# q/k projections of an attention image moved into the image itself, and another split of one convolution tile

## The chip, the cores and the metric

One core of a Trainium2 chip runs the whole kernel. The metric is device time in microseconds (us) of one execution; a run is several executions, and the median stands for them. The engines are called by the profile's names: PE (TensorE matmuls), PEld (its weight loads, which lie beside the matmuls), DVE (VectorE), ACT (ScalarE), POOL (GpSimd) and SP (SyncE, here only a DMA queue).

## The reference, cut to what matters

The input x has 16 images of 384 channels and 32 x 32 pixels. Each image passes two residual layers, all in float32:

```
x = x + attention(groupnorm(x))      # 8 heads of 48, over 1024 pixels; q, k, v, proj
x = x + dwconv7x7(groupnorm(x))      # one symmetrised 7x7 filter per channel
```

Attention is softmax(q kT / sqrt(48)) v for each head, and a projection with a bias. The convolution has 49 taps per channel, with a border of three zeros. Group norm works over 32 groups of 12 channels.

## The kernel before, in words

**Tiles.** An image is three tiles of 128 channels x 1024 pixels (k = 0, 1, 2). Heads go in four pairs (u = 4b + 0..3). For three pairs q and k are projected directly: qk_step(b, t, s) runs twelve float32 matmuls for pair t and s = 0 (q) or 1 (k) into a PSUM buffer (L415), and ACT copies it to the tile qk (L422). The fourth pair is gathered from spare rows of the first three by six SP DMAs (qk_rest, L431). In the profile each float32 matmul has two records.

**Blocks.** The main loop walks an image in eight blocks of eight steps (r = 0, 8, ..., 56; 16 steps are a pair). A block is eight s_steps (scores, L466, and the exp on ACT, L474), then a middle, then eight av_steps (L482) and one ACT copy of the accumulator (take, L493). Values v (v_step, L441) are projected in the middle of the block r = 0; the output projection of the image in front (project, proj_step, L535) follows there. The instruction streams of all engines are in order.

**Order.** A planner in Python writes the order: clock is PE's planned time, vclock that of DVE. catch_up(to) puts DVE work (convolution taps, and delayed calls of after(wait, cost, f)) into the stream until vclock reaches clock. act_slot(free) puts ACT work that is due (a first-in first-out list, applies) into the stream if its cost fits. other(done, scores_next) stands in the middle and at the end of each block and places a projection or q/k chunks. Due times are planned, not measured: an engine that gets there early waits.

**Images.** There is one x buffer (xpool, bufs = 1). begin_x(b + 1) loads the next image into it once the last reader of image b is in the stream: before, that is the last v_step, since q and k of image b were all projected during image b - 1 (`queue(b + 1)`, chunks 0 and 1 behind project, the others at fixed blocks). x_apply normalises the three tiles in place on ACT (L332), and had its place in the middle of project.

**Convolution.** x1_chains(b, st) normalises the attention's output (xn, L332) and starts its taps: one scalar_tensor_tensor on DVE per tap and tile (conv_tap, L600), up to three tiles in turn. Four of the last six tiles go to PE instead: PE_TILES = (14, 2), (14, 1), (15, 2), (15, 1). Each of their halves (16 image rows, 512 columns) is two pieces of 28 matmuls (conv_on_pe, L705) in four groups of 32 output channels; it reads two shifted copies sh that eight DMAs bring back from DRAM (conv_load, L682), issued by SP and ACT in turn. conv_on_pe_end adds the PSUM buffer to DVE's sum (L720), and a POOL DMA writes it out (L613). The tile SHARED = (14, 1) is divided: DVE takes the upper half, PE the lower one (h = 1). So PE's convolution is seven half tiles, in this order, here H1 to H7: (14,2) h0 and h1, (14,1) h1, (15,2) h0 and h1, (15,1) h0 and h1. The copies sh live in the pool qkpool (five buffers, one of them for a weight matrix), so a half's two copies are loaded when the half two places in front of it has been computed. PSUM tiles of this kind come from a pool of three (ps_s). Tile (15, 0), LONE, stays on DVE with two sums in turn (sum2) that are added at the end (L860).

**The two ends.** At the start eight warm matmuls of 384 columns (L1045) run on PE before the statistics of image 0 are averaged there (groups_on_pe, L301, two rounds); then x is normalised (L328 and L332) and all six qk_steps of image 0 follow. At the end come the last divisions (L563, L564), projection (L572), residual (L581), group norm on PE, and the convolution pieces.

Of the kernel before, what the change touches and what calls it, by code (L numbers as in the profile page):

```python
# [13 lines left out]
ALU = mybir.AluOpType  # L14
# [30 lines left out]
def kernel(  # L45
# [64 lines left out]
    def run(general):  # L110
        tag = "g" if general else "f"
        with ExitStack() as stack:
# [20 lines left out]
            def psum(name):  # L133
                return ps_s.tile([P, 2, HALF], F32, tag="s", name=name)
# [4 lines left out]

            PE_TILES = [(b, k) for b in (B - 2, B - 1) for k in PE_K]  # L140
            SHARED = None if general else (B - 2, PE_K[1])
            LONE = (B - 1, 0)

            def flat(t):
# [2 lines left out]
            def halves(t):  # L147
                return t.rearrange("p (h n) -> p h n", h=2)
# [444 lines left out]
            def conv_tap(b, k, dy, dx, dst=None):  # L593
                (oy, iy), (ox, ix) = region(dy, dx)
                if (b, k) == SHARED:
                    oy = slice(oy.start, min(oy.stop, H // 2))
                    iy = slice(iy.start, oy.stop - oy.start + iy.start)
                dst = x1s[b, k] if dst is None else dst
                acc = dst.rearrange("p (h w) -> p h w", w=W)[:, oy, ox]
                nc.vector.scalar_tensor_tensor(  # L600
                    acc,
                    xn1s[b, k].rearrange("p (h w) -> p h w", w=W)[:, iy, ix],
                    wsym[:, k, dy + PAD, dx + PAD : dx + PAD + 1],
                    acc,
                    ALU.mult,
                    ALU.add,
                )
# [84 lines left out]
            def conv_on_pe(b, k, h, part):  # L692
                if (b, k) not in pss:
                    pss[b, k] = psum(f"ps_conv_{b}_{k}")
                order = sorted(
                    ((d0, dx) for d0 in range(2) for dx in range(-PAD, PAD + 1)),
                    key=lambda t: t[1] != 0,
                )
                for n, (d0, dx) in enumerate(order):
                    if n // KS != part:  # L700
                        continue
                    _, (ox, ix) = region(0, dx)
                    for i in range(SH):
                        src = shs[b, k, h, i // 2][:, i % 2, 0 : ROWS * W]
                        nc.tensor.matmul(  # L705
                            pss[b, k][CH * i : CH * (i + 1), h, :].rearrange(
                                "p (y x) -> p y x", x=W
                            )[:, :, ox],
                            lhsT=mats[k][:, i, d0 * KS + dx + PAD, :],
                            rhs=src.rearrange("p (y x) -> p y x", x=W)[  # L710
                                :, SH * d0 : SH * d0 + H // 2, ix
                            ],
                            start=(n == 0),
                            stop=(n == len(order) - 1),
                        )

            def conv_on_pe_end(b, k):
                h = slice((b, k) == SHARED, 2)
                dst = halves(x1s[b, k])[:, h]
                nc.vector.tensor_tensor(dst, pss.pop((b, k))[:, h], dst, ALU.add)  # L720
                conv_end(b, k)

            def exact_step(u, i):
# [95 lines left out]
            def us_tap(dy, dx):  # L819
                late_us = 0.02 if clock > last_image else 0.0  # L820
                rows = H - abs(dy)
                if tuple(active[0][0:2]) == SHARED:
                    rows = H // 2 - max(0, -dy)
                return (rows * (W - abs(dx)) + (128 if len(active) > 1 else 268)) / 955 + late_us

            def tap():
# [60 lines left out]
            def issue(c):  # L887
                nonlocal clock
                kind, b, i = c
                if kind == "qk":  # L890
                    qk_step(b, *divmod(i, 2))
                    clock += US_QK
                elif kind == "rest":
                    qk_rest(b)
                else:
                    v_step(b, i)
                    clock += US_V
                    if i == NT // 2 - 1 and b + 1 < B:
                        begin_x(b + 1)

            lims = []

            applies, pending = deque(), []
            ON_VECTOR = (B - 2,)

            def project(b):
                nonlocal clock
                for o in range(NK):
                    proj_step(b, o)
                    clock += US_PROJ  # L910
                    if b in ON_VECTOR:
                        after(8.0, 1.3, lambda o=o: x1_part(b, o))

                    if o == 1 and pending:
                        pending.pop()()
                if b not in ON_VECTOR:
                    after(1.6, 0.2, lambda: x1_means(b))
                if chunks and b + 2 in ready:

                    issue(chunks.popleft())  # L920
                    catch_up(clock)
                    act_slot(9.0)
                    issue(chunks.popleft())

            def x1_part(b, k):
# [40 lines left out]
            def act_slot(free):  # L966

                while applies and applies[0][0] <= clock and applies[0][1] <= free:
                    _, cost, f = applies.popleft()
                    free -= cost  # L970
                    f()
# [20 lines left out]
            def begin_x(b):  # L992
                load_x(b)
                if b == 1:
                    after(10.0, 3.8, lambda: x_channels(b))
                else:
                    pending.append(lambda: x_apply(b, None))

            def x_channels(b):
                st = Stats(f"x_{b}")  # L1000
# [34 lines left out]
                if p == NP - 1:  # L1035
                    proj.append((now() + 7.0, b))

            def queue(b):
                chunks.extend(("qk", b, i) for i in range(6))
                chunks.append(("rest", b, 0))  # L1040


            warm = psum("warm")
            for n in range(8):
                nc.tensor.matmul(  # L1045
                    warm[:, n % 2, 0:C], lhsT=v[:, n, 0:P], rhs=v[:, n, 0:C], start=True, stop=True
                )
# [8 lines left out]
            conv_weights()  # L1056
            means_of(st.bs, x_mean[:, 0, :])
            ready[0] = 0.0
            queue(0)
            every = [(b, k) for b in range(2, B) for k in range(NK)]  # L1060
            for n, bk in enumerate(every):
                after(3.0 * n, 0.0, lambda bk=bk: stream_in(*bk))
# [42 lines left out]
            def conv_piece():  # L1105
                nonlocal clock
                b, k, h, part = pe_conv.popleft()
                while (b, k, h, 1) not in shs:
                    loads(1)
                conv_on_pe(b, k, h, part)  # L1110
                clock += 6.2
                if part == 1:
                    loads(2)
                if (h, part) == (1, 1):
                    after(6.0, 1.2, lambda: conv_on_pe_end(b, k))

            def other(done, scores_next):

                catch_up(clock)
                if proj and proj[0][0] <= clock:  # L1120
                    project(proj.popleft()[1])
                elif scores_next and chunks:
                    kind, cb, i = chunks[0]
                    first = {"qk": 2 * NT * (i // 2), "rest": 2 * NT * 3}[kind]
                    if ready.get(cb, 1e9) <= clock and done >= first:

                        act_slot(9.0)
                        issue(chunks.popleft())
                        if kind == "qk":
                            issue(chunks.popleft())  # L1130
                catch_up(clock)

            def fast_finish(b):
# [27 lines left out]
            for b, n0, size in [  # L1161
# [2 lines left out]
                r = n0 - b * PER_B  # L1164
                if n0 == NS - PER_B:
                    last_image = clock
                if r == 0:
                    while chunks:
                        issue(chunks.popleft())
                    if b + 1 < B:  # L1170
                        queue(b + 1)
                for n in range(n0, n0 + size):
                    s_step(n)
                clock += (size * US_STEP + US_TURN) / 2
# [4 lines left out]
                if ending:  # L1179
                    catch_up(clock)  # L1180
                    divide_at_once(NP * b + NP - 1, 0)
                    vclock += 4.2
                    for o in range(NK):
                        proj_part(b, o, (0, 1))
                    clock += 2 * US_PROJ
                else:
                    catch_up(clock)
                    act_slot(4.5)
                    other(r + size, False)
                for n in range(n0, n0 + size):  # L1190
                    av_step(n)
                    u, h, i = n // (2 * NT), n // NT % 2, n % NT
# [5 lines left out]
                if ending:  # L1198
                    catch_up(clock)
                    assert not invs and not waiting  # L1200
                    fast_finish(b)
                else:
                    other(r + size, True)
                if b == B - 4 and r == 32:
                    after(0.0, 2.0, check_early)
                if b == 1 and r == 0:
# [88 lines left out]
```

## Time and profile before

| | us |
|---|---|
| median of 6 runs | 2933.49 |
| lowest and highest | 2931.82, 2935.51 |
| profiled execution | 2933.9 |
| its span, first to last instruction | 2932.0 |
| PE busy in it | 2910.4 (99%) |
| DVE busy | 2559.7 (87%) |
| ACT busy | 1434.0 (49%) |
| POOL busy | 192.6 (7%) |

A busy PE row says only that one matmul or another was under way; its ends are modelled. The mean granted PE clock is 0.996 of full speed. In the timeline a row is a merged group: its start, its length, the engine, the line, the operands, how often (x), and in brackets the idle time before it and what ended it. In the view by stages each engine has its busy time and, in brackets, its instructions; PEclk is the granted clock.

### The profile page before, as it was taken

The numbers are of one execution on the slowest core, as the hardware profiler recorded it, in microseconds if no ns is written. First come the engines' busy times: TensorE is split into PE (matmuls) and PEld (weight loads), VectorE is DVE, ScalarE is ACT, GpSimd is POOL, SyncE is SP. The second block draws the span as 40 slices with busy tenths as digits, with TensorE's granted clock in tenths as the row PEclk, the third lists the DMA queues.
The fourth block names the chain that finished last, engine by engine and source line by source line (L and its number), as shares of the span: only waits on it lengthen the run. The fifth ranks groups of instructions, "written<-read, shape, count | busy, mean of one in ns | idle before, by whom it ended". The sixth has DMA issues, their size and how long they took to land.

```text
span 2932.0 us, 30301 instructions
## 1 busy us (share of the span) xinstructions
PE 2910.4 (99%) x11562; PEld 1175.5 (40%) x11562; DVE 2559.7 (87%) x2565; ACT 1434.0 (49%) x1713; POOL 192.6 (7%) x305
## 2 busy tenths in 40 slices
PE   8999999999999999999999999999999999999998
PEld 4334343433434334343433434334343433434333
DVE  4500998989989898998989999898998999899997
ACT  2544545555454554545454454555445465454610
POOL 2213000010000001000000000001000000100000
PEclk9999999999999999999999999999999999999999
DMA  6513121121212112121121213013121221202324
GB/s 230 182 25 66 24 66 38 32 73 26 57 37 67 37 34 73 24 64 37 49 56 27 57 37 74 30 34 78 25 58 37 55 49 27 69 25 53 108 60 117
DMA packets 72540, 169.86 MB, mean 58 GB/s; under 512 B 30416, under 2 KB 32352, under 8 KB 70848
## 3 DMA queue, kind: packets, MB, share of 16 engines
q0 software_dynamic: 29456, 96.10, 12.0%
q1 hardware_dynamic: 41168, 68.12, 9.6%
q10 hardware_dynamic: 1760, 3.61, 0.5%
q8 instruction: 93, 1.52, 0.2%
q14 instruction: 63, 0.52, 0.1%
HBM read 119.93 MB, written 29.36 MB: 51 GB/s over the span
## 4 chain that ended last, share of the span: by engine, by line
PE 86%; DVE 7%; issue 5%; DMA 1%; POOL 0%; ACT 0%; POOLq 0%; SPq 0%; DVEq 0%; ACTq 0%
PE ps_s L466 27%; PE acc L482 27%; PE ps_qk L415 16%; PE ps_v L441 8%; PE ps_proj L535 7%; DVE x L600 6%; DVE sum L600 1%; PE warm L1045 0%; DVE o L518 0%; DMA out<-x 0%; DMA inv<-inv 0%; DMA gr_x<-af_x 0%; DVE bs_x L233 0%; PE ps_st_x L301 0%; ACT sq_x L264 0%
## 5 line engine op out<-in xcount | busy, mean ns | idle before, releaser
L600 DVE SCALAR_TENSOR_TENSOR x<-xn,wsym,x 128x899 f32<-128x899 f32 (+11 forms) x2181 | 2352.4, 1152 | 147.6 <-ACT xn L332 147.6
L474 ACT ACTIVATE e<-ps_s 128x1024 f32<-128x1024 f32 x1024 | 952.4, 1051 | 53.7 <-PE ps_s L466 50.8
L466 PE MATMUL ps_s<-qk 48*128 48x512 f32 x4096 | 914.2, 596 | 0.0
L482 PE MATMUL acc<-e,v 128*64 128x512 f32 x4096 | 907.2, 595 | 0.0
L466 PEld LDWEIGHTS ps_s<-qk 48*128 48x128 f32 x4096 | 376.5, 185 | 533.8 <-ACT e L474 257.7
L482 PEld LDWEIGHTS acc<-e,v 128*64 128x64 f32 x4096 | 282.9, 137 | 608.3 <-issue 603.7
L415 PE MATMUL ps_qk<-x,wqk 128*128 128x512 f32 x1152 | 507.2, 597 | 2.4 <-DVE x L328 2.4
L493 ACT COPY o<-acc 128x512 f32<-128x512 f32 x128 | 75.2, 588 | 672.8 <-PE acc L482 672.8
L415 PEld LDWEIGHTS ps_qk<-x,wqk 128*128 128x128 f32 x1152 | 217.0, 191 | 289.0 <-issue 286.5
L441 PE MATMUL ps_v<-wv,x 128*128 128x384 f32 x768 | 252.0, 488 | 0.0
L535 PE MATMUL ps_proj<-o,wp 128*128 128x512 f32 x540 | 234.2, 592 | 0.0
L422 ACT COPY qk<-ps_qk 128x1024 f32<-128x1024 f32 x96 | 96.8, 1009 | 257.9 <-PE ps_qk L415 257.9
L441 PEld LDWEIGHTS ps_v<-wv,x 128*128 128x128 f32 x768 | 144.6, 190 | 109.7 <-ACT e L474 12.1
L535 PEld LDWEIGHTS ps_proj<-o,wp 128*128 128x128 f32 x540 | 102.6, 190 | 125.9 <-issue 120.3
L450 ACT COPY v<-ps_v 128x384 f32<-128x384 f32 x128 | 55.1, 483 | 185.5 <-PE ps_v L441 185.5
L154 POOL DMA_DIRECT2D x<-in_x x42 | 22.3, 538 | 1645.6 <-PE ps_v L441 1608.3
L543 ACT ACTIVATE x<-ps_proj,bp 128x1024 f32<-128x1024 f32 x45 | 50.1, 1114 | 135.2 <-PE ps_proj L535 135.2
L518 DVE TENSOR_TENSOR o<-o,inv 128x1024 f32<-128x1024 f32 x63 | 76.8, 1218 | 37.6 <-DMA inv<-inv 34.9
L332 ACT ACTIVATE xn<-x,sc_x 128x1024 f32<-128x1024 f32 x46 | 53.8, 1235 | 87.7 <-DMA sc_x<-gr_x 63.8
L705 PE MATMUL ps_conv<-sh,mat 128*32 128x480 f32 (+3 forms) x784 | 83.1, 580 | 0.2 <-DMA sh<-xd 0.2
L507 DVE RECIPROCAL rec<-sums 128x16 f32<-128x16 f32 x63 | 15.4, 244 | 72.4 <-DMA sums<-sum 72.4
L355 DVE BATCH_NORM_STATS2 bs_all<-xs 128x6 f32<-128x512 f32 x84 | 51.7, 680 | 11.7 <-DMA xs<-in_x 11.7
(113 smaller groups left out, 522.0 us busy)
## 6 DMA issues: line engine op xcount, KB each, us to landing
x<-in_x POOLq DMA_DIRECT2D x90, 512.0 KB, 5.3
inv<-inv SPq DMA_DIRECT2D x126, 256.0 KB
out<-x POOLq DMA_DIRECT2D x48, 512.0 KB, 3.8
xs<-in_x POOLq DMA_DIRECT2D x42, 512.0 KB, 6.3
qk<-qk SPq DMA_DIRECT2D x96, 128.0 KB
o<-o SPq DMA_DIRECT2D x90, 64.0 KB
sh<-xd SPq DMA_DIRECT2D x34, 160.0 KB
sh<-xd ACTq DMA_DIRECT2D x22, 160.0 KB
```

What stands on the lines that cost most here:

```text
L415: nc.tensor.matmul(ps[:, h, :], lhsT=wqk[:, k, s, t, :], rhs=xns[b][:, k, h * HALF : (h + 1) * HALF], start=(k == 0), stop=(k == NK - 1),)
L422: nc.scalar.copy(halves(qks[u][:, s, :]), ps)
L441: nc.tensor.matmul(ps[:, j, 0:C], lhsT=xns[b][:, k, t * P : (t + 1) * P], rhs=wv[:, k, :], start=(k == 0), stop=(k == NK - 1),)
L450: nc.scalar.copy(dst.rearrange("p (h d) -> p h d", d=D + 1)[:, :, 0:D], ps[:, j, 0:C].rearrange("p (h d) -> p h d", d=D),)
L466: nc.tensor.matmul(ps[:, j, :], lhsT=qks[u][r, 1, i * P : (i + 1) * P], rhs=qks[u][r, 0, h * HALF : (h + 1) * HALF], start=True, stop=True,)
L474: nc.scalar.activation(es[n], ps, AF.Exp, scale=SCALE)
L482: nc.tensor.matmul(accs[u, h][64 * j : 64 * j + 64, :], lhsT=v_of(u, i, j), rhs=e[:, j, :], start=(i == 0), stop=(i == NT - 1),)
L493: nc.scalar.copy(os_[u][:, h * HALF : (h + 1) * HALF], accs.pop((u, h)))
L518: nc.vector.tensor_tensor(os_[u], os_[u], invs.pop(u), ALU.mult)
L535: nc.tensor.matmul(ps[:, h, :], lhsT=wp[:, t, o * P : (o + 1) * P], rhs=os_[NP * b + t][:, h * HALF : (h + 1) * HALF], start=(t == 0), sto ...
L600: nc.vector.scalar_tensor_tensor(acc, xn1s[b, k].rearrange("p (h w) -> p h w", w=W)[:, iy, ix], wsym[:, k, dy + PAD, dx + PAD : dx + PAD + 1],
L705: nc.tensor.matmul(pss[b, k][CH * i : CH * (i + 1), h, :].rearrange("p (y x) -> p y x", x=W)[:, :, ox], lhsT=mats[k][:, i, d0 * KS + dx + ...
```

## The change

Three things are changed.

1. **q and k.** A chunk is now one pair (both qk_steps). Only pair 0 of image b + 1 is projected during image b, from the block that ends at step 40 on. Pair 1 is projected in its own image, behind project (image 0: at the end of the block r = 0), and pair 2 at the end of the block r = 8. qk_rest and begin_x(b + 1) come behind pair 2, so the next image's load moves from behind v_step to there, and x_apply from the middle of project to the first slot from 7.0 us (planned) after that. Between the two steps of each pair there are now a catch_up and an act_slot. Image 0 starts its scores after pair 0 alone; image 15 now holds two pairs.
2. **The shared tile.** SPLIT = 24: DVE's taps on tile (14, 1) cover 24 of its 32 image rows instead of 16, and PE's pieces of H3 the last 8 rows, so its matmuls have 256 columns (less at the sides) instead of 512. Their number, 56, and the loads of sh stay. The last add covers 256 columns. The planned time of a piece of H3 is 3.2 instead of 6.2.
3. **Warm-up.** Four warm matmuls instead of eight.

```diff
+            SPLIT = 3 * H // 4
...
                 if (b, k) == SHARED:
-                    oy = slice(oy.start, min(oy.stop, H // 2))
+                    oy = slice(oy.start, min(oy.stop, SPLIT))
...
+                y0 = SPLIT - H // 2 if (b, k) == SHARED else 0
...
-                            )[:, :, ox],
+                            )[:, y0:, ox],
                             lhsT=mats[k][:, i, d0 * KS + dx + PAD, :],
                             rhs=src.rearrange("p (y x) -> p y x", x=W)[
-                                :, SH * d0 : SH * d0 + H // 2, ix
+                                :, SH * d0 + y0 : SH * d0 + H // 2, ix
                             ],
...
-                h = slice((b, k) == SHARED, 2)
-                dst = halves(x1s[b, k])[:, h]
-                nc.vector.tensor_tensor(dst, pss.pop((b, k))[:, h], dst, ALU.add)
+                c = slice(SPLIT * W if (b, k) == SHARED else 0, N)
+                dst = x1s[b, k][:, c]
+                nc.vector.tensor_tensor(dst, flat(pss.pop((b, k)))[:, c], dst, ALU.add)
...
                 if kind == "qk":
-                    qk_step(b, *divmod(i, 2))
-                    clock += US_QK
-                elif kind == "rest":
-                    qk_rest(b)
+                    act_slot(9.0)
+                    for s in range(2):
+                        qk_step(b, i, s)
+                        clock += US_QK
+                        if s == 0:
+
+                            catch_up(clock)
+                            act_slot(9.0)
+                    if i == NK - 1:
+                        qk_rest(b)
+                        if b + 1 < B:
+                            begin_x(b + 1)
                 else:
                     v_step(b, i)
                     clock += US_V
-                    if i == NT // 2 - 1 and b + 1 < B:
-                        begin_x(b + 1)
...
-                    if o == 1 and pending:
-                        pending.pop()()
...
-                if chunks and b + 2 in ready:
-
-                    issue(chunks.popleft())
-                    catch_up(clock)
-                    act_slot(9.0)
+
+                if chunks and chunks[0] == ("qk", b + 1, 1):
                     issue(chunks.popleft())
...
-                    pending.append(lambda: x_apply(b, None))
+                    applies.append((now() + 7.0, 3.7, lambda: x_apply(b, None)))
...
+            for b in range(B):
+                chunks.extend(("qk", b, t) for t in range(NK))
...
-            for n in range(8):
+            for n in range(4):
...
-            queue(0)
+            issue(chunks.popleft())
...
-                clock += 6.2
+                clock += 3.2 if (b, k) == SHARED else 6.2
...
-                    kind, cb, i = chunks[0]
-                    first = {"qk": 2 * NT * (i // 2), "rest": 2 * NT * 3}[kind]
-                    if ready.get(cb, 1e9) <= clock and done >= first:
-
-                        act_slot(9.0)
+                    _, cb, t = chunks[0]
+                    when = PER_B * cb + (-24, 8, 16)[t]
+                    if ready.get(cb, 1e9) <= clock and done >= when:
                         issue(chunks.popleft())
-                        if kind == "qk":
-                            issue(chunks.popleft())
...
-                if r == 0:
-                    while chunks:
+                if r % (2 * NT) == 0 and r // (2 * NT) < NK:
+                    while chunks and chunks[0][1:] <= (b, r // (2 * NT)):
                         issue(chunks.popleft())
-                    if b + 1 < B:
-                        queue(b + 1)
```

## The prediction

> **What bounds the kernel now.** I read the page first, then PE's waits, then the timelines of the first 60 us, of one image in the middle and of the last 110 us, and there the view of the loads.
>
> ```profile
> span 2932.0 us, 30301 instructions
> PE 2910.4 (99%) x11562; PEld 1175.5 (40%) x11562; DVE 2559.7 (87%) x2565; ACT 1434.0 (49%) x1713; POOL 192.6 (7%) x305
> ```
>
> ```profile
> PE warm L1045 <- POOL v L181: 5.1, 1, 5.1
> PE ps_qk L415 <- DVE x L328: 2.4, 1, 2.4
> PE ps_st_x L301 <- DVE d_x L316: 1.3, 2, 0.6
> PE ps_conv L705 <- DMA sh<-xd: 0.2, 1, 0.2
> PE ps_proj L572 <- DVE o L564: 0.2, 1, 0.2
> ```
>
> These are all of PE's waits (total, number, longest). None lies between 18.9 and 2826 us: PE runs without a gap through all sixteen images. Moving q/k work among images leaves its sum alone and can't win time there; it can only lose some if a gap opens. What can be won lies before 18.9 us, and in the tail, by taking matmuls away. In the middle DVE has room:
>
> ```profile
> 1691.80 3.68 DVE L600 SCALAR_TENSOR_TENSOR x<-xn,wsym,x 128x1024 f32<-128x1024 f32 x3 [9.87 <-ACT xn L332]
> ```
>
> The bracket is the idle time before the row: DVE has ended one image's taps 9.87 us before the next may begin. It is not behind.
>
> **The start.**
>
> ```profile
> 8.95 0.17 DVE L310 COPY mn_x<-st_x 128x3 f32<-128x3 f32 x1
> 9.07 2.87 PEld L1045 LDWEIGHTS warm<-v 128*128 128x128 f32 x9 [0.30 <-issue]
> 12.40 1.62 PE L301 MATMUL ps_st_x<-mn_x,masks 128*128 128x1 f32 x14
> 18.90 33.14 PE L415 MATMUL ps_qk<-x,wqk 128*128 128x512 f32 x72 [2.38 <-DVE x L328]
> 52.08 1.01 ACT L422 COPY qk<-ps_qk 128x1024 f32<-128x1024 f32 x1 [4.14 <-PE ps_qk L415]
> ```
>
> The means are ready at 9.12; L301 starts at 12.40, behind the warm matmuls. Weight loads come every 0.64 us up to 9.07, then nine in 2.87, so every 0.32. Eight records fewer are 8 x 0.32 = 2.56 us, and L301 could start at 9.8. Everything up to 18.90 is a chain behind it (PE, DVE, POOL, DVE), and the weights have landed by 14.3 (the view of transfers shows none from then to 19), so the first q/k matmul comes 2.56 earlier. Bounds: 2.9 at most, where DVE's means set it; at worst -0.6, if the shorter warm-up leaves PE at half clock for L301. The row for that is L301's second round in the tail, 3.06 for 14 loads instead of 1.64, twice 1.4 against the 2.2 still won.
>
> The clock matters again at 18.9:
>
> ```profile
> 16.20:22.80 6.60, 4.22 (x7) 2.07 (x8) 4.11 (x11) 1.24 (x1) 4.36 (x7) 0.50 0.54 180
> 2839.00:2845.60 6.60, 6.50 (x34) 4.04 (x38) 3.35 (x6) 1.24 (x1) 2.61 (x2) 0.50 0.14 32
> ```
>
> The 0.50 is the granted clock: after a spell of little PE work it is half for some 6.8 us. The first q/k matmuls lose about 2 us by that in either kernel; I take no difference (bounds 0.4 won, 1.4 lost). The Trainium skill ("TensorE: Matmul & The Clock Gate", Part 1: The HAM clock gate) says that full clock is granted after about 3.4 us of sustained work, counted in free-running windows. Four matmuls at 1.28 us are 5.1 us, which need not hold a whole window; by that rule the warm-up's gain is lost in part of the executions, and an estimate of its mean is half the 2.56. The trace shows full clock from 9.3, 4.2 us after the first, on which I rely.
>
> New: with pair 0 alone, the first score waits for ACT's copy of k. Before, PE went from q/k (whose last matmul ends at 52.04) straight to scores, since four more steps had covered the copy of pair 0. Now 0.1 + 1.01 + 0.05 = 1.15 us of PE idle, once (bounds 1.0 to 1.6). And one more place where q/k stands between av and scores: groups behind a change of kind take 10.50 instead of 10.30, so 0.2. The start gives 2.56 - 1.15 - 0.2 = 1.2.
>
> **The middle: nothing.** Pair 1 stands behind project and pair 2 at the end of the block r = 8, where two pairs stood before; pair 0 follows block r = 32. The same matmuls, moved some blocks. SP's six qk_rest DMAs and the three loads of x move too. POOL then waits for pair 2's matmuls; ahead of it are the statistics' transfers and the outputs, which are out by then. SP's next transfer behind qk_rest is the inverse for pair u0, which may come some us late; DVE waits for it, and its 9.87 us cover that. x_apply falls in the middle of the block r = 16, between exps and take:
>
> ```profile
> 1694.28 7.44 ACT L474 ACTIVATE e<-ps_s 128x1024 f32<-128x1024 f32 x8
> 1707.31 0.59 ACT L493 COPY o<-acc 128x512 f32<-128x512 f32 x1 [5.59 <-PE acc L482]
> ```
>
> ACT idles 5.59 there, and three normalisations take 3.50. In this image's numbers: q/k ends at 1693.2, three issues take 1.6, the page's median from issue to landing is 5.3, so x is there at 1700.1, before the exps end at 1701.7. ACT could start as late as 1703.8. Cost nothing; without that cover every us later is a us for each of 14 images.
>
> **The tail.** Two pairs (20.8 us of PE) now lie in image 15, so image 14 ends that much earlier against the tail, and its taps begin earlier. DVE pays for the shared tile: a tap of 899 elements takes 1.14, one of 464 0.69, so 1.03 ns an element; 8 rows x 30.3 columns are 242 elements, 0.25 us, times 49 = 12.2 us. This is under 20.8: hidden. What DVE must still do is LONE.
>
> ```profile
> 2861.68 3.51 SPq L682 DMA_DIRECT2D sh<-xd  x4
> GB/s 455 164 0 0 0 0 0 187 91 182 307 387 355 194 182 273 250 194 193 182 125 262 307 330 239 228 239 193 319 228 194 114 46 34 34 23 59 23 0 0
> 2868.78 1.21 DVE L720 TENSOR_TENSOR x<-ps_conv,x 128x1024 f32<-128x1024 f32 x1
> 2872.77 0.19 PE L1091 MATMUL ps_again<-lim,ones 128*1 128x2 f32 x2
> 2911.21 1.23 DVE L860 TENSOR_TENSOR x<-x,sum 128x1024 f32<-128x1024 f32 x1
> 2919.57 1.23 DVE L720 TENSOR_TENSOR x<-ps_conv,x 128x1024 f32<-128x1024 f32 x1 [7.13 <-PE ps_conv L705]
> ```
>
> DVE ends LONE at 2912.4 and waits 7.13 us for PE: PE sets the end. H2 ends at 2861.68 (SP is released), H3 at 2872.77: 11.1 us. With 256 columns H3 takes 5.55, if streaming sets the pace: 112 groups of weight load and matmul in 5.55 are 50 ns each. Against it stands L301, 116 ns a pair, but with weights of 128 columns; the upper bound is H3 as long as before. The skill (same page, Back-to-back issue gap) gives 81 ns for load and matmul at 128 columns, an estimate of 9.1 us for H3, which would win 2.0 there instead of my term; no row here shows such a short one.
>
> Now what is late next. H4 needs two things that come after H2's end, and H3's length hid both. Its sh copies are issued at 2861.68; the row in GB/s (40 slices of 0.225 us from 2861) has its last bytes at 2869.5, so 7.9 us; the same view for the others gives 7.5 and 6.9. And H4's PSUM tile is the fourth claim on three buffers: it waits for DVE's add of tile (14, 2), 2868.78 to 2869.99. So H4 starts 8.0 to 8.8 after H2's end, not 5.6; I take 8.5. Won: 2872.8 - 2870.2 = 2.6 (bounds 1.5, and 5.5 if neither waits), with 2.9 us of PE idle. Whether DVE's divisions come a little late behind longer taps (L572 waits 0.2 today): 0.3, bounds -0.2 and 1.0.
>
> **Sum.** 2.56 - 1.15 - 0.2 + 2.6 - 0.3 = 3.5 us. The profiled execution took 2933.9, so 2930.4; it is 0.4 above the median of 2933.49, so 2930.0.
>
> **Rivals.**
>
> *Neither load nor add holds H4.* Then the tail gives 5.5, and the sum 6.4: 2927.1. For it: four loads ranged from 6.9 to 7.9 and DVE may do the add earlier. Against: both must fall by over 1 us. 18%.
>
> *The idle PE loses its clock.* At 2839 5 us of little work did it; a gap of 1.1 us at 2849.6 didn't. Here 2.9 us lie between. Half clock for 3.4 to 6.8 us costs 1.7 to 3.4: 2932.5. 17%.
>
> *DVE becomes the end.* If the taps of image 14 don't begin earlier, LONE ends at 2912.4 + 12.2 = 2924.6, against 2920.8 today: 2937.3, as a bound. Against: 20.8 over 12.2. 4%.
>
> *Slower: x lands late between exps and take.* From 1703.8 on, that is 10.6 us after pair 2's last matmul, ACT holds up the exps and PE waits, in 14 images. One us over it makes 2944. Against: 3.7 us of margin on median transfers. It also stands for any stall that repeats for each image. 8%.
>
> **Numbers.** The forecast has 53% (own range 2927.7 to 2932). A measurement of this kernel tells 0.2%, 5.87 us, from no change. Faster by more is under 2927.6: the first rival, 18%. Within: 53 + 17 + 4 = 74%. Slower: 8%. The range leaves out the slower rival and the extremes: 2926 to 2934.
>
> **What would show it.** L301 starting near 9.8 and L415 near 16.3; one gap of 1.2 us before the first score and none up to the tail; the taps of image 14 ending before LONE's; H3 5.6 us, then a PE wait for sh or for L720; LONE ending some 8 us ahead of PE. Wrong: a PE wait that repeats 14 times, half clock over L301 at the start, or H4 following H3 at once.

## The result, and the profile after

The changed kernel takes 2940.22 us (median of 17 executions, 2937.89 to 2947.31); the kernel before, in the same session, 2933.21 (37 executions, 2931.76 to 2935.56). The ratio is 1.0026, interval [1.0020, 1.0032]: slower by 0.26%, where 2930.0 was forecast. The profiled execution took 2939.85, 5.95 more than that of before, and its span is 5.8 longer.

The head of the changed kernel's page:

```profile
span 2937.8 us, 30304 instructions
PE 2908.3 (99%) x11554; PEld 1178.2 (40%) x11554; DVE 2572.5 (88%) x2565; ACT 1436.3 (49%) x1713; POOL 193.4 (7%) x305
```

DVE is busier by 12.8 us, near the 12.2 that were worked out for the shared tile. PE is *less* busy, and the span longer, so waits were added. PE's waits (total, number, longest), new or grown ones only:

```profile
PE ps_proj L573 <- DVE o L565: 4.3, 1, 4.3
PE ps_conv L707 <- DVE good L1095: 1.4, 1, 1.4
PE ps_s L467 <- ACT qk L423: 1.1, 1, 1.1
PE ps_proj L536 <- DMA o<-o: 0.8, 3, 0.3
```

The second and third line were forecast. The first is the old 0.2 of the last division, grown to 4.3. Behind it, in the timeline of PE and in the view by stages (the 0.50 is the granted clock):

```profile
2832.62 7.25 PE L573 MATMUL ps_proj<-o,mat 128*128 128x512 f32 x10 [4.25 <-DVE o L565]
2831.30:2838.00 6.70, 5.38 (x7) 2.29 (x8) 5.68 (x7) 0.00 (x0) 0.00 (x0) 0.50 0.00 0
```

The same row of before:

```profile
2826.33 4.56 PE L572 MATMUL ps_proj<-o,mat 128*128 128x512 f32 x10 [0.19 <-DVE o L564]
```

These ten matmuls took 4.56 before and take 7.25 here: the wait was followed by half the clock, and that costs another 2.7.

Set against the trace of before, the 5.8 us divide so. The first L573 comes 2.2 later (2803.82 against 2801.60). Of this, 2.1 is lost in the images: from one image's first v_step to the next, six images are 0.2 to 0.8 longer than 175.1, 2.4 in sum, where before had 0.3. The other 0.1 is the start, which wins nothing. The late division adds 4.1, the half clock 2.7. The convolution of the tail gives back 3.3, the rest is 0.1. This is the account of one execution, which lies near the median; where the others lose their time no trace shows.

### The profile page after: what moved, and what is told of

It reads as the page before. It is cut to its first block, busy times and chain, and to the rows that moved or that the text cites. A ratio compares the mean times of both kernels' runs of the same rounds, so it can differ in the third digit from the quotient of the medians.

```text
span 2937.8 us, 30304 instructions
## 1 busy us (share of the span) xinstructions
PE 2908.3 (99%) x11554; PEld 1178.2 (40%) x11554; DVE 2572.5 (88%) x2565; ACT 1436.3 (49%) x1713; POOL 193.4 (7%) x305
## 5 line engine op out<-in xcount | busy, mean ns | idle before, releaser
L551 POOL DMA_DIRECT2D x<-in_x x45 | 39.2, 870 | 1865.5 <-ACT x L544 1732.3
L707 PE MATMUL ps_conv<-sh,mat 128*32 128x480 f32 (+7 forms) x784 | 78.3, 553 | 1.4 <-DVE good L1095 1.4
```

The lines of the kernel that those rows point to most:

```text
L707: nc.tensor.matmul(pss[b, k][CH * i : CH * (i + 1), h, :].rearrange("p (y x) -> p y x", x=W)[:, y0:, ox], lhsT=mats[k][:, i, d0 * KS + dx ...
```

## Why the last division is late

The same view of DVE in both kernels, first before, then after. In brackets is the idle time ahead of the row:

```profile
2567.33 3.68 DVE L600 SCALAR_TENSOR_TENSOR x<-xn,wsym,x 128x1024 f32<-128x1024 f32 x3 [10.52 <-ACT xn L332]
2822.14 3.35 DVE L563 RECIPROCAL inv<-ps_sum 128x512 f32<-128x512 f32 x1
```

```profile
2547.86 3.68 DVE L601 SCALAR_TENSOR_TENSOR x<-xn,wsym,x 128x1024 f32<-128x1024 f32 x3 [4.58 <-ACT xn L333]
2565.94 1.23 DVE L519 TENSOR_TENSOR o<-o,inv 128x1024 f32<-128x1024 f32 x1 [3.91 <-DMA inv<-inv]
2738.36 1.23 DVE L519 TENSOR_TENSOR o<-o,inv 128x1024 f32<-128x1024 f32 x1 [2.58 <-DMA inv<-inv]
2828.43 3.35 DVE L564 RECIPROCAL inv<-ps_sum 128x512 f32<-128x512 f32 x1
```

The first row of each is where the taps of image 13 begin: the last time that DVE has to wait for new work. From there to the last division its stream is full, and every wait in it comes out at the end. Before, DVE needed 2822.14 - 2567.33 = 254.8 us from there to the last L563, with 1.2 of waits; after, it needs 280.6, with 3.91 + 0.28 + 2.58 = 6.8. It begins 19.5 earlier (image 14's two pairs, moved behind) and needs 25.8 more: 5.5 of this is waits for the inverse, the rest is work, the longer taps of the shared tile among it, that the planner put there. So DVE is 6.3 later and PE 2.2, which leaves the 4.1.

The inverse (the factors of a division, sent through DRAM: inv<-rec, then the gathers inv<-inv) is late because of qk_rest. SP's rows of the last image:

```profile
2718.43 9.14 SPq L432 DMA_DIRECT2D qk<-qk  x6
2727.67 0.53 SPq L510 DMA_DIRECT2D inv<-rec  x1
2733.64 1.12 SPq L513 DMA_DIRECT2D inv<-inv  x2
```

The six copies of qk_rest are issued over 9.14 us, since they wait for ACT's copies of pair 2; the inverse stands behind them, though its input (rec) was there at 2726.57 (2726.34 + 0.23). DVE takes the division up at 2738.36.

The place in the queue of issues is the smaller part of it. In images 1 to 15 the first pair's inv<-rec is issued at most 1.1 us after its input is there. What grows is the time from there to the gathers, which wait for it to land: 7.2 to 10.4 us in images 1 to 14 and 5.97 in the last, where nearly all other pairs have 1.42, and so have the first pairs of images 1 to 14 in before. So the transfer itself is slow there, with the copies of qk_rest in front of it and, up to image 14, the load of the next x under way. Whether it stands behind the copies or is slowed by what runs beside it was not told apart.

## The experiments

At the beginning two theories stood against each other: qk_rest in front of the inverse on SP makes the division late, by itself; or the longer taps on the shared tile are too much for DVE, by themselves. After the first runs they became one: the inverse is late, and the longer taps leave DVE no room to make up for it. The rivals: VectorE becomes the end; transfers of the first images collide. Later came one of the prediction's own rivals, x landing late. Each run is set against before on the same chip; the interval is of the ratio.

### Each part alone

q and k moved, the shared tile divided as before, eight warm matmuls:

```diff
-            SPLIT = 3 * H // 4
+            SPLIT = H // 2
...
-                clock += 3.2 if (b, k) == SHARED else 6.2
+                clock += 6.2
...
-            for n in range(4):
+            for n in range(8):
```

> The changed kernel with SPLIT back at 16 rows and eight warm matmuls: only the q/k part is left. In the changed kernel's trace DVE's last division comes 4.5 us after its sums are ready and PE waits 4.25 for it. Theory 1 (late inverse): SP's six qk_rest transfers stand in its queue until pair 2 is copied, so the inverse for the first pair of each image comes late, DVE waits for it, and in image 15 nothing takes the delay up. That needs no shared tile: PE waits about 4 us again before the last projection, its clock halves once more there, and the time is 2939 to 2944. Theory 2 (too much for DVE): the 12.2 us of further taps in image 15 put DVE behind. Then the wait is gone here, and the time is the one before plus 1.2 (first copy) and 2 (small gaps in the images): 2935 to 2937.

2939.29 (2937.21 to 2943.01), ratio 1.0017 [1.0008, 1.0026]. The last division is not late here. The timeline of DVE has

```profile
2829.34 3.36 DVE L564 RECIPROCAL inv<-ps_sum 128x512 f32<-128x512 f32 x1 [3.11 <-PE ps_sum L562]
```

DVE waits for PE there, since its shorter taps have run out. So the late inverse alone doesn't make the last division late; that form of the theory fell. Its time does not fit the other theory either, which gave 2935 to 2937. Of the 7.1 us by which its profiled execution is longer than that of before, 4.4 lie in image 1: 2.9 in this wait of PE, and 1.5 for a half clock of 3.4 us behind it. PE's timeline:

```profile
219.37 15.82 PE L536 MATMUL ps_proj<-o,wp 128*128 128x512 f32 x33 [2.93 <-DMA o<-o]
```

Most of the rest lies in the start: the first scores come at 33.49, 2.3 later than in the changed kernel with its four warm matmuls.

The kernel before with the new division of the shared tile (and its planned 3.2), nothing else:

```diff
+            SPLIT = 3 * H // 4
...
-                    oy = slice(oy.start, min(oy.stop, H // 2))
+                    oy = slice(oy.start, min(oy.stop, SPLIT))
...
```

> The kernel before with the shared tile's new split alone. Theory 1: DVE isn't late for the last division (PE waits under 1 us), H3 takes 5.5 us, H4 waits for the add and starts some 8 us after H2's end, 3 us won on PE; but the taps of image 14 don't begin earlier here, so DVE ends its lone tile up to 12.2 us later, at up to 2924 of the span, and the time is 2931 to 2938. Theory 2: DVE is late for the last division by 4 us or more as in the changed kernel, and PE waits for it: 2938 to 2942.

2938.78 (2937.3 to 2939.9), ratio 1.0016 [1.0007, 1.0025]. PE waits 1.1 for the last division, and DVE sets the end, as its timeline shows:

```profile
2923.43 1.20 DVE L722 TENSOR_TENSOR x<-ps_conv,x 128x1024 f32<-128x1024 f32 x1
2924.57 1.20 DVE L862 TENSOR_TENSOR x<-x,sum 128x1024 f32<-128x1024 f32 x1
```

The last row is LONE's final add, behind PE's last half tile; in the other kernels it lies well ahead of that. So the shared tile's longer taps need the room that the moved q and k give at the end: the prediction's third rival ("DVE becomes the end", 2937.3 as a bound) holds without that move. Each part alone costs some 5 us, each in another place.

The kernel before with four warm matmuls:

```diff
-            for n in range(8):
+            for n in range(4):
```

> The kernel before with four warm matmuls instead of eight. The changed kernel's trace starts its first q/k matmul 1.85 us earlier, but then runs 5.0 us at half clock instead of 4.0, so 1.35 is left. Both theories: 0.5 to 2 us faster than before, 2931 to 2933. If the shorter warm-up is what makes the run to run spread larger, the runs of this one spread by more than 4 us.

2933.74 (2933.01 to 2934.44), ratio 0.9999 [0.9990, 1.0008]. Nothing is won, though PE reaches the last projection 1.2 us earlier (its first L572 at 2800.37, 2801.60 before). PE's waits have

```profile
PE ps_proj L572 <- DVE o L564: 1.7, 1, 1.7
```

DVE was a second bound all along, 0.2 us behind PE: the 0.2 in the list of before was the sight of it.

### Taking the causes out

The copies of qk_rest 20 planned us later, so that the inverse is in front of them:

```diff
-                        qk_rest(b)
+                        after(20.0, 0.0, lambda: qk_rest(b))
```

> The changed kernel with qk_rest put 20 us (planned) later into the stream, when pair 2 has long been copied: SP's queue no longer stands in front of the first pair's inverse. Theory 1: DVE's waits for inv fall from 96 us to under 50, the small gaps in front of project go, DVE is at most 1.5 us late for the last division, PE's clock stays full there: 2930 to 2934. Theory 2: no change at the end, PE still waits some 4 us for the last division: 2938 to 2940.

2936.01 (2933.15 to 2938.69), ratio 1.0007 [0.9998, 1.0016]; 4.2 under the changed kernel, but 2 above what was expected. DVE's waits for the inverse fall from 96 to 43 us in all. Its timeline, to be held against that of after:

```profile
2549.91 3.68 DVE L601 SCALAR_TENSOR_TENSOR x<-xn,wsym,x 128x1024 f32<-128x1024 f32 x3 [9.20 <-ACT xn L333]
2737.04 1.23 DVE L519 TENSOR_TENSOR o<-o,inv 128x1024 f32<-128x1024 f32 x1 [2.39 <-DMA qk<-qk]
2827.12 3.34 DVE L564 RECIPROCAL inv<-ps_sum 128x512 f32<-128x512 f32 x1
```

DVE's slack ahead of image 13's taps is 9.2 again instead of 4.6, and the waits behind it are 0.51 + 0.50 + 2.39 = 3.4, which is 3.4 less than after. From the first row to the last L564 (2827.12) DVE needs 277.2, which is 3.4 less than the 280.6. PE waits 1.24 there instead of 4.25, and the clock stays whole at that place. Nearly all of the 3.4 is image 14's wait (3.91, now 0.51); the last image's hardly moves (2.58, now 2.39), though the inverse is now issued at once. From the issue of inv<-rec to the gathers it still takes 4.8 to 5.6 us in images 2 to 15. So, at the last division, the theory holds in its joint form: late inverse and full DVE. What the edit does to the median is not this alone, for it clears another place too: in its trace ACT never waits for the next image's x, and in the changed kernel's it does in eight images (see below).

The changed kernel with 4 planned us of taps held back in the last image:

```diff
+                if b == B - 1 and r == 40:
+                    vclock += 4.0
```

> The changed kernel with 4.0 us added to DVE's planned time in image 15 (behind the block r = 40), so that some four taps fewer stand in front of the last divisions and as many more behind them. In its trace DVE ends its lone tile 12 us before PE, so the taps can wait. Theory 1 (DVE is late there, and this lateness is the price): PE's wait for the last division falls from 4.25 to under 0.6 us, the clock stays full before H1 (2.7 us), so 5 to 7 us less than the changed kernel: 2933 to 2935. Rival (PE is held in the tail by the loads or the add instead, and would wait there for as long): 2938 to 2940.

2939.61 (2936.11 to 2944.47), ratio 1.0021 [1.0012, 1.0030]. The wait of L573 falls from 4.25 to 1.06 and the half clock there is gone, and yet the median is within some 0.6 of the changed kernel's; 2933 to 2935 was expected. Its profiled execution (span 2934.3) is its fastest, with a granted clock of 0.997, where the others have 0.994 to 0.996; in it image 1 is 3 us longer. This is a miss for the median: the place is right in the trace, but in most executions something still loses as much, and no trace shows what. How much of the median's loss the last division makes is therefore not shown.

The kernel before with four warm matmuls and 2 planned us held back:

```diff
-            for n in range(8):
+            for n in range(4):
...
+                if b == B - 1 and r == 40:
+                    vclock += 2.0
```

> The kernel before with four warm matmuls and 2.0 us held back in front of the last divisions. With four warm matmuls alone PE was 1.2 us earlier up to the last divisions and waited 1.74 for DVE there, nothing gained. If DVE is the second bound at that place, 0.2 us behind PE, the wait is under 0.3 here and 0.8 to 1.8 us are won: 2932 to 2933. If not, 2933.7 as without.

2932.18 (2930.23 to 2933.24), ratio 0.9993 [0.9984, 1.0002]. PE's 1.7 us for the last division is gone, and the median is 1.6 under that of the warm-up alone. The interval still holds 1.

### What is left: image 1, and x

All three pairs of image 1 projected during image 0, and the load of image 2's x behind image 1's values, as they stood before:

```diff
-                        if b + 1 < B:
+                        if b + 1 < B and b != 1:
                             begin_x(b + 1)
...
+                    if b == 1 and i == NT // 2 - 1:
+                        begin_x(b + 1)
...
-                    when = PER_B * cb + (-24, 8, 16)[t]
+                    when = PER_B * cb + ((-24, -16, -8) if cb == 1 else (-24, 8, 16))[t]
```

> The changed kernel, but all three pairs of image 1 are still projected in image 0, so that image 0 ends later. Theory 3 (collision): in two traces PE waits 3 us before the first project, since the sums of image 0's last pair take 10 us to DRAM and back beside the scatter of the group statistics (gr_all), which ran before image 0's end in the kernel before. Then this wait is gone here in every execution, the runs spread less (under 5 us instead of 9.4), and the median falls by 1 to 3 us: 2937 to 2939; the late last division stays. Rival (the wait comes from the late inverse of the first pair): no change, 2940.

2942.05 (2940.88 to 2944.65), ratio 1.0028 [1.0017, 1.0040]. Its trace has no stall at the first project, as expected, but then the changed kernel's own trace had none either. PE waits 4.8 for the last division, with its half clock, and the time does not fall: a miss, 3 above what was expected. By itself this repairs nothing that the changed kernel's median shows.

The three edits together, that is qk_rest 20 planned us later, image 1's pairs early, and 2 planned us of taps held back:

> Three amendments on the changed kernel: qk_rest 20 us later, the three pairs of image 1 in image 0, and 2.0 us held back in front of the last divisions. By the ledger of the traces only the start (about 0.2 won), H3 (3.2 won) and small terms are left against the kernel before: 2929 to 2931. If it is over 2932, a cost of moving q and k is left that I have not named.

2944.10 (2939.73 to 2946.60), ratio 1.0035 [1.0021, 1.0049]: a miss, slower than any of its parts. There is no late division in its trace, but two new stalls, of 6.3 us at 461 and 4.0 at 993, half clock included. POOL, SP, ACT and PE around the first:

```profile
447.44 1.62 POOL L155 DMA_DIRECT2D x<-in_x  x3 [7.24 <-PE ps_qk L416]
448.26 3.93 SPq L432 DMA_DIRECT2D qk<-qk  x6
464.20 1.24 ACT L333 ACTIVATE x<-x,x_sc 128x1024 f32<-128x1024 f32 x1 [3.22 <-DMA x<-in_x]
466.89 7.72 PE L467 MATMUL ps_s<-qk 48*128 48x512 f32 x20 [2.89 <-ACT e L475]
```

The inverse (its two gathers at 447.04), x and qk_rest now go out between 447 and 452, and x's last tile is not there until 464.20, 16.8 us after the first issue. ACT stands in x_apply, the exps queue behind it, and PE waits for an exp. In the changed kernel the gathers of the inverse were issued at 457.22, when ACT was already at work on x, and ACT waited for nothing at that place. This is the prediction's slower rival, x late between exps and take, though not in every image.

In the changed kernel's own trace x is late as well, but PE does not pay for it. ACT waits for x in eight of fourteen images; the longest is this:

```profile
1332.87 1.24 ACT L333 ACTIVATE x<-x,x_sc 128x1024 f32<-128x1024 f32 x1 [1.01 <-DMA x<-in_x]
1334.50 2.54 ACT L333 ACTIVATE x<-x,x_sc 128x1024 f32<-128x1024 f32 x2 [0.40 <-DMA x<-in_x]
1337.44 0.59 ACT L494 COPY o<-acc 128x512 f32<-128x512 f32 x1 [0.39 <-PE acc L483]
```

ACT is 1.4 us late here and still 0.39 ahead of the take, so 0.39 is what is left of the margin. With the taps held back ACT waits up to 2.9 us in one image (0.70, 0.58 and 1.60, from 809 to 814), and PE's scores behind that take 7.37 instead of 7.14. In the trace of before, and with qk_rest later, it does not wait for x at all. So x late may be a part of what the executions without a trace lose; that is argued, not shown.

So four kernels were run that differ only in two edits, image 1's pairs early or not, and x_apply in its place or half a block later (some 14 us):

```diff
-                    applies.append((now() + 7.0, 3.7, lambda: x_apply(b, None)))
+                    applies.append((now() + 20.0, 3.7, lambda: x_apply(b, None)))
```

All four have qk_rest later and 2 planned us of taps held back; one of them is the run just shown, five executions.

> The changed kernel with the copies of the third pair's halves (qk_rest) 20 planned us later, and 2 planned us of taps held back in the last image. Division theory: the first edit alone left 1.24 us of wait for the last division at a median of 2936.0, the second takes that wait; it gives 2934 to 2935.5 and no wait of the project for the last division. Collision theory: the stall of 3.1 us in image 1 stays, for neither edit touches it. X theory: a wait of ScalarE for x can still come in some images, so runs spread over 4 us and more. Rival: holding taps back only moves the wait to the end of the kernel, where VectorE would be last; it gives 2936 and LONE behind PE's last half tile.

> The same two edits as in the run before this one, and the ScalarE work on x half a block later. X theory: no wait for x in any image, a narrower spread of runs (under 4 us) and 0.5 to 2 us less than without it: 2932.5 to 2934.5. Division theory alone: the same as without it within 0.5 us. This is the version in which the causes named so far are out, save the stall in image 1 (3.1 us), which would be left as the whole of what is lost against 2930.

> The run with all three edits (qk_rest 20 planned us later, all pairs of image 1 projected in image 0, 2 planned us of taps held back; 2944.1, with two stalls of 6.3 and 4.0 us in its trace), and the ScalarE work on x half a block later. X theory: both stalls were ScalarE waiting for x in front of a take, and both go with the half clock behind them: 2931 to 2934, and the spread of runs falls under 4 us. Rival: the late x is only a symptom of transfers that are slow in that place; something else waits for them instead (the next pair's q/k, the halves of qk_rest, the inverse), and the time stays over 2940.

| median us (ratio to before) | x_apply in its place | half a block later |
|---|---|---|
| image 1 as in the change | 2933.40 (1.0001 [0.9992, 1.0010]) | 2934.53 (1.0006 [0.9997, 1.0015]) |
| image 1's pairs early | 2944.10 (1.0035 [1.0021, 1.0049]) | 2929.55 (0.9984 [0.9975, 0.9993]) |

The second row decides for x: 14.6 us between two kernels that differ only in when ACT asks for it. In the last kernel the transfers lie as in the three edits together, but ACT asks later and has x without a wait:

```profile
447.75 1.62 POOL L155 DMA_DIRECT2D x<-in_x  x3 [7.24 <-PE ps_qk L416]
448.57 4.07 SPq L432 DMA_DIRECT2D qk<-qk  x6
469.95 3.55 ACT L333 ACTIVATE x<-x,x_sc 128x1024 f32<-128x1024 f32 x3
```

The first row shows that in the other arrangement x was not late: there the inverse's gathers and qk_rest are issued at 455.98 and 457.20, and ACT has x (issued at 449.03) at 457.09 without a wait. Which of the two transfers holds x up was not told apart. Against my expectation, x later wins nothing there, and the executions spread over 9.0 us instead of under 4. The second column gives image 1 as 5.0 us. In the trace, the time from image 0's first v_step to image 2's is 339.5 us with image 1 as in the change and 335.4 with its pairs early, and in all three kernels with the early pairs it is between 335.3 and 335.5; in the others it ranges from 335.4 (the changed kernel) to 341.7.

The last kernel is 4.6 us faster than before (2934.12 on that chip), and its executions lie within 2.6 us (2928.16 to 2930.72), where those of the changed kernel spread over 9.4. It beats both kernels.

And the changed kernel with x_apply later alone:

> The changed kernel with one edit: the ScalarE work on the next image's x (three ACTIVATE of 128x1024, 3.55 us together) is put half a block later (some 14 us), behind the exps of the block's second half. X theory: x lands 8.5 us and more after its issue and in some images only behind those exps, ScalarE then waits in front of the take, and the scores behind it wait too (two stalls of 6.3 and 4.0 us in the trace of the run with all three edits); that is what is left of the loss in the middle. It gives 2935 to 2938, no score that waits for an exp, and the late last division (4.2 us and 2.7 us of half clock) as in the changed kernel. Division theory alone: what is lost is lost at the last division, the middle's stalls are no part of the median; it gives 2939 to 2941. Against both: the three ACTIVATE now stand between the second half's exps and its take, and if x was never late this changes nothing but where the 3.55 us lie.

2947.15 (2945.09 to 2952.16, five executions), ratio 1.0048 [1.0034, 1.0062]: a clear miss, 7 above the changed kernel. The span is 6.1 longer than the changed kernel's, and image 1 alone 6.3 (341.7); the rest cancels: the late division is there as before (4.3). In image 1 two chains of small transfers come late, one for the first project (2.2), one for the third pair's copies, which ACT makes behind a normalisation that waits for its factors:

```profile
272.03 3.50 ACT L333 ACTIVATE xn<-x,sc_x 128x1024 f32<-128x1024 f32 x3 [8.52 <-DMA sc_x<-gr_x]
```

Neither is touched by the edit. Why they are longer in this trace than in the changed kernel's, and whether they are what its other executions lose, is left open.

## Why the prediction was wrong, point by point

- **The inverse: the step that failed.** "DVE waits for it, and its 9.87 us cover that." The 9.87 is real, and through most images the late inverse does eat into it (4.58 of 10.52 is left at image 13). But it is idle time ahead of the next image's taps, and a wait is only made good if such a place lies behind it. Behind image 13's there is none. 5.5 us more of waits in images 14 and 15 (6.8 against 1.2) went straight to the last division.
- **The last division: the term that was mis-sized.** It was 0.3, bounds -0.2 and 1.0. It measured 4.1 in the trace, with 2.7 of half clock behind it. The 12.2 us of longer taps, "under 20.8: hidden", was right for the end of the kernel (DVE waits 11.9 for PE there, 7.1 before), wrong for the last division: the planner fills DVE up to it by planned times, so the 8.6 us left over are not in front of it. The 0.2 in the list of before's waits should have been read as a second bound, as the warm-up run shows. Its weight in the median stays open, since the median hardly moved when the taps were held back.
- **The middle: nothing.** It was 2.4 in the profiled execution, in six images, where before had 0.3; partly a project that waits for the fourth pair's half (o<-o, 0.8). With the inverse in front of qk_rest 0.5 is left, image 1 apart. In image 1 there is more, up to 6.3, in other arrangements. The "3.7 us of margin" for x were not there: forecast were 6.9 us from the first issue of x to its landing, and in one image ACT has the last two tiles only 10.9 us after it (1323.61 to 1334.50). That PE lost nothing by it in this trace was luck.
- **The start** was to give 1.2 and gives nothing: the first scores come 20.78 earlier (31.20 against 51.98), and the two pairs that went to the last image cost 20.87 there. The timeline of PE:

```profile
9.40 1.62 PE L302 MATMUL ps_st_x<-mn_x,masks 128*128 128x1 f32 x14
11.66 3.01 PE L302 MATMUL ps_st_x<-d_x,masks 128*128 128x1 f32 x14 [0.64 <-DVE d_x L317]
```

  L302 came at 9.40 (9.8 was forecast), but its second round ran at half clock, 3.01 instead of 1.87: in this execution the clock fell at 11.84 instead of 16.1, and stayed so for 10.2 us instead of 6.8. So q and k began at 17.05, not 16.3, and their first 5.0 us ran at half clock (4.0 before). The bound of "at worst -0.6" named this. The wait for k's copy was 1.10 (1.15 forecast).
- **H3 and H4: right.** H3's loads come as fast as was worked out, 98 in 5.07 us, 52 ns each (50 forecast, and not the 81 that the prediction set beside it; PEld):

```profile
2871.15 5.07 PEld L707 LDWEIGHTS ps_conv<-sh,mat 128*32 128x32 f32 x98 [0.26 <-issue]
2878.44 46.22 PE L707 MATMUL ps_conv<-sh,mat 128*32 128x512 f32 x448 [1.38 <-DVE good L1095]
2877.16 1.22 DVE L722 TENSOR_TENSOR x<-ps_conv,x 128x1024 f32<-128x1024 f32 x1
2911.64 1.23 DVE L862 TENSOR_TENSOR x<-x,sum 128x1024 f32<-128x1024 f32 x1
```

  (PEld, PE and DVE of the changed kernel.) H4 waited for the add of tile (14, 2) (the row at 2877.16; the view names the small one behind it), as forecast, and began 7.8 us after H2's end, instead of 8.5. It won 3.3, forecast 2.6. LONE ended at 2912.9, 12 us ahead of PE's last half. With the late division, the small gaps, the late x and image 1's collisions taken out, the whole gives 4.6 us against the 3.5 of the sum.
- **The rivals.** Slower had 8%, by x late in every image. What came was slower, in the trace by another mechanism. x late is real: it takes 6.3 us from PE at one place of another arrangement, and in the change's own trace it uses up the margin but nothing more. "The idle PE loses its clock" came true at the last division, not at H4, where PE idled for 1.4 us and the clock stayed whole. The gap of 1.1 us at 2849.6 that this rival was weighed with is one of weight loads; PE's own row there has 0.19. "DVE becomes the end" does come, when the shared tile is changed alone.

## What to carry to other kernels

Slack covers a late wait only if it lies behind it on the same engine: find the last place where the engine waits for new work, and count every wait behind that in full. A bracket of 0.2 us before the last step named, in this kernel, a second engine that was just as late; a gain on the first was worth nothing until the second had room. Where transfers on several queues were kept apart only by when their issuers got there, moving one of them moves the meeting point. Asking for the data later took out 14.6 us in one arrangement, and nothing in another, so look in the trace which of them you have. And one profiled execution is one draw: an edit that mends it can leave the median where it was.

## What the runs showed of the hardware that was not expected

- **The clock's price of a wait is a matter of luck between 2 and 3 us.** PE idle for 4.25 us (the changed kernel) and 2.89 (the three edits together) was followed by half clock for 6.8 us, 2.93 (q and k alone), 2.04 (x_apply later) and 2.03 (the three edits, at 997) by 3.4. But 3.13 (qk_rest later, at the first project) was not, nor 2.31 (taps held back) or 2.20 (x_apply later), nor any of 1.1 to 1.4. All half-clock stretches that end in work, in all fourteen traces, are 3.4, 6.8 or 10.2 us long. The one at the start is 6.8 in the three traces with eight warm matmuls; with four it is 6.8 in seven and 10.2 in four. The Trainium skill ("TensorE: Matmul & The Clock Gate", Part 1: The HAM clock gate) gives free-running windows of about 3.4 us and half clock after an idle one; the lengths agree, and so does it that the same wait is priced in one run and not in another, but 2.0 us of idle, less than a window, could be enough here.
- **Small transfers get slow in company.** The first step of the inverse's way through DRAM (inv<-rec issued, to the gathers inv<-inv issued) takes 1.42 us for most pairs in both kernels, and 7.2 to 10.4 for the first pair of images 1 to 14 of the changed one, behind the copies of qk_rest and beside the load of x. With qk_rest put behind it, it is 4.8 to 5.6 in images 2 to 15, so the copies are a part of the cause and not all of it. The round trip of a pair's sums through DRAM (sum<-o issued, to sums<-sum issued) took 1.6 us in image 0 of the kernel before (212.84 to 214.42), 6.4 in the changed kernel, and 10.7 with x_apply later (191.50 to 202.24), where it lies beside the scatter of the statistics (gr_all, issued from 176 to 181, waited for until 202). That these meet is seen; that one slows the other was not tried by itself.
